# Strassen's scheme for one more stage of a two-layer graph network, its sums of the matrix made in an earlier stage, and another order of products in the last stage

## The chip, the cores and the metric

The kernel runs on one core of one Trainium2 chip. The metric is the device time of one execution in microseconds; "before" is the median of three runs. The profile is one further execution, recorded by the hardware profiler. TensorE (PE in the profile) does matmuls, VectorE (DVE) and ScalarE (ACT) read its results from PSUM, and DMAs are issued from the queues of SyncE (SP), GpSimd (POOL) and ScalarE.

## The reference

Two layers of graph convolution with a residual and a layer norm each. N is 2048 nodes, the batch is 8, and there are 64 features in and out. The weights of each node are mixed from 16 pools by its embedding. Cut to what matters:

```python
def layer0(x, A, emb, weight, bias):
    w = einsum('nd,dkio->nkio', emb, weight); b = emb @ bias
    As = [eye(N), A, 2.0 * (A @ A) - eye(N)]
    x_g = einsum('knm,bmc->bnkc', stack(As), x)
    return einsum('bnki,nkio->bno', x_g, w) + b

def layer1(x, emb, A, weights, bias):
    support = [eye(N), A, 2.0 * A @ A - eye(N),
               softmax(relu(emb @ emb.T), axis=1)]
    ...   # the same two einsums with four supports

x = layernorm(x + layer0(x, adj, ...))
x = layernorm(x + layer1(x, adj, ...))
```

## The kernel before

**Stages.** The work is cut into 40 stages: five phases of eight, each stage for a block of 256 nodes (two slabs of 128). Stage n = 8 i + j is phase i, block j. A0 is u = A x in layer 0, B0 is A u; A1, Z1 and V1 are A x, softmax times x, and A u in layer 1. Stage 8 is thus the first of B0 and stage 32 the first of V1. "Layer 1's s" in the short name of this change is the result of A u there. x and u stay in SBUF, as 16 slabs of 128 nodes by 512 columns (batch times feature). In layer 1, u of a block is stored to memory (`store_u`) and comes back before V1 (`load_u`), since the room of u holds other sums until then.

**Products.** A stage's product is plain or by Strassen's scheme (the variant of Winograd); the set `plain` says which. Plain: 64 units of work; a unit is 128 rows by 128 by 256 columns, and each fp32 matmul of the source is two instructions in the profile. In V1 and B0 the plain form (`turned`) has u stationary and 256 columns of the matrix moving. Strassen (`strassen`): the block of the matrix is cut in four quarters A11 to A22 (slab of rows by parity of the column slab), u or x in four quarters B11 to B22 (parity of slab by left or right half of its columns). Seven products of eight units each make 56 units. In V1 and B0 each product is 32 instructions of 128 moving columns. They are:

```text
p1 = A11 B11   p2 = A12 B21   p3 = (A12-S2) B22   p4 = A22 T4
p5 = (A21+A22) T1   p6 = S2 T2   p7 = (A11-A21) T3     S2 = A21+A22-A11
T1 = B12-B11   T2 = B22-T1   T3 = B22-B12   T4 = T2-B21
c00 = p1+p2   c10 = p1+p6+p7-p4   c11 = p1+p6+p7+p5   c01 = p1+p6+p5+p3
```

c00 and c01 belong to the stage's first slab (slab 0), c10 and c11 to its second (slab 1). Products go to one of two accumulator banks in turn, and a bank is free when the adds that read it are done. The order of products is 1, 4, 7, 2, 6, 5, 3 in every stage.

**Sums.** T1 to T4 are made by VectorE from all slabs of u or x at once, once per phase (`Sums.make`, five operations of 128x2048 or shorter ones). T2 is made in the place of B12. The sums of the quarters of the matrix are made once per block: in stages of A0 with Strassen by `sum_of_a`, and where an A0 stage is plain and its sums are needed later, by `sums_of_a` (four pieces of four VectorE operations of 128x256, and a store of 512 KB on SP for each). Both are stored in `sd` and loaded by later stages. Before, A0's blocks 0 and 1 are plain, as is block 0 of B0, A1 and V1; so only block 1 needs `sums_of_a`.

**Order.** The order of the work around the products is written out by hand: `put(n, place, f, ...)` hangs a call into stage n at a place from 0 to 64, scaled to the stage's length (64 or 56 units); `spread` distributes a list over places. When the product generator has come to a place, the calls are emitted, and every engine works through its instructions in the order of emission. Into each stage's product go: `weights` (matmuls pw, whose results ScalarE and VectorE copy to `w`), `apply` of the stage before (four of them, 32 matmuls po each, for four groups of 32 nodes; the instructions in the profile are twice as many; VectorE accumulates each in four operations by a mask), `post` (mean, square, deviation, scaling, and the output DMA; `post(0)` to `post(2)`), `turn`, loads and stores. The applies of a stage need its result t, in V1 those of slab 1 (2 and 3) first. In the last stage, 39, there is no stage behind: `apply(2)` is at place 60, and 3, 0 and 1 follow behind the products with all of `post`.

**Matrix loads.** `Ahead` keeps four 512 KB buffers of the matrix loaded in the order in which the products use them; each `next()` fills one and takes one. Weights have three such buffers. Both are issued on SP's queue, where an issue that waits for a buffer holds those behind it.

Of the kernel before, what the change touches and what calls it, by code (L numbers as in the profile page):

```python
# [15 lines left out]
P = 128  # L16
# [32 lines left out]
def two_graph_layers(ctx: ExitStack, tc: tile.TileContext, x, x_t, adj_b, adj_q, layers, out):  # L49
# [167 lines left out]
        for q in range(4):  # L217
            pool.dma_start(out=s1[q * D:(q + 1) * D, :].bitcast(F32), in_=estk[1][(q // 2) * D:(q // 2 + 1) * D, :])

    plain = {("A0", 1)} | {(phase, 0) for phase in ("A0", "B0", "A1", "V1")}  # L220

    class Ahead:

# [16 lines left out]
    def load_adj(t, key):  # L240
# [6 lines left out]
        else:  # L247
            sp.dma_start(out=t, in_=src.rearrange("p k n -> p (k n)"))


    lefts = [("quarter", (0, 0)), ("quarter", (1, 1)), ("sum", 2), ("quarter", (0, 1)), ("sum", 1), ("sum", 0), ("sum", 3)]
    quarters = [("quarter", at) for at in ((0, 0), (1, 1), (1, 0), (0, 1))]
    adj = Ahead(4, lambda: stream.tile([P, 4 * NB], F32, tag="a", name="a"), load_adj,
                [key for phase in ("A0", "B0", "A1", "V1") for j in range(NBLK)
                 for key in ([("plain", j, i) for i in range(NJ // 4)] if (phase, j) in plain
                             else [(kind, j, i) for kind, i in (quarters if phase == "A0" else lefts)])])
# [5 lines left out]
    class Stage:  # L262
# [152 lines left out]
        def product(self):  # L415
            if self.wide:
                if self.j % 2 == 0:
                    self.rest = self.pair[1].rest = self.strassen(X)
                    return islice(self.rest, self.length)
                return self.rest  # L420
            if self.phase == "Z1":
                return self.turned(X, self.softmax())
            if self.kk:
                return self.turned(U, self.loaded()) if self.plain else self.strassen(U)
            if self.n == 0:
                self.slabs = U[0:SB]
# [9 lines left out]

        def loaded(self):
            for _ in range(NJ // 4):
                a = adj.next().rearrange("p (m n) -> p m n", n=NB)
                yield [a[:, i, :] for i in range(4)]  # L440

        def accumulator(self, name):
# [15 lines left out]
            self.store_u()  # L458

        def store_u(self):  # L460
            if self.kk == 0:
                for s in range(SB):
                    (sp if self.li else pool).dma_start(out=ud[self.j][:, s, :], in_=self.slabs[s])

        def strassen(self, right):
# [4 lines left out]
                      "B22": lambda k: right[2 * k + 1][:, half:BC]}  # L470
            for i in range(4):
                rights[f"T{i + 1}"] = lambda k, i=i: sums[i](k)
            if self.wide:
                p1, p4, v = (four.tile([P, BC], F32, tag="f2k", name="temp") for _ in range(3))
                mine = {f"A{h + 1}{t + 1}": self.pair[h].quarters[t] for h in range(2) for t in range(2)}
            else:
                temps = one.tile([P, 4, half], F32, tag="wsplit", name="temps")
                p1, p4, v = (temps[:, i, :] for i in range(3))
                mine = {}
            made = {}  # L480
# [4 lines left out]
            def quarter(name):  # L485
                if streamed:
                    mine[name] = adj.next()
                    adj.held += 1
# [6 lines left out]
            def times(name, what, left):  # L495
                made[name] = acc = self.accumulator(name)[:, 0:2 * nodes]
                a = (mine[left] if inside else adj.next()).rearrange("p (k n) -> p k n", n=nodes)
                for k in range(k_slab):
                    if self.kk:
                        for q in range(2):  # L500
                            pe.matmul(acc[:, q * nodes:(q + 1) * nodes], rights[what](k)[:, q * P:(q + 1) * P],
                                      a[:, k, :], start=(k == 0 and q == 0), stop=(k == k_slab - 1 and q == 1))
                            yield nodes / NB
                    else:
                        pe.matmul(acc, a[:, k, :], rights[what](k), start=(k == 0), stop=(k == k_slab - 1))
                        yield 1
                if inside and name in ("p7", "p6", "p5", "p3"):
                    if streamed:
                        adj.held -= 1
                        adj.fill()  # L510
                    self.used(what)

            def add(dst, a, b, op=ALU.add):

# [4 lines left out]
                else:  # L519
# [4 lines left out]
                    for par in range(2):  # L524
                        of = lambda x: x[64 * par:64 * par + 64, :].rearrange("p (q n) -> p n q", n=nodes)
                        dve.tensor_tensor(to[:, :, 4 * dst[1] + par:4 * dst[1] + par + 3:2], of(a), of(b), op=op)

            if inside:
                quarter("A11")
                quarter("A22")  # L530
            yield from times("p1", "B11", "A11")
            act.copy(p1, made["p1"])
            if inside:
                quarter("A21")
                sum_of_a(2, "A11", "A11", "A21", ALU.subtract)
                sum_of_a(0, "A21", "A21", "A22", ALU.add)
            yield from times("p4", "T4", "A22")
            self.used("T4")
            act.copy(p4, made["p4"])
            if inside:  # L540
                quarter("A12")
                sum_of_a(1, "A22", "A22", "A11", ALU.subtract)
            yield from times("p7", "T3", "A11")
            add(v, made["p7"], p1)
            add(p4, v, p4, ALU.subtract)
            yield from times("p2", "B21", "A12")
            add((0, 0), made["p2"], p1)
            if inside:
                sum_of_a(3, "A12", "A12", "A22", ALU.subtract)
            yield from times("p6", "T2", "A22")  # L550
            add(v, made["p6"], v)
            add(p1, made["p6"], p1)
            add((1, 0), made["p6"], p4)
            yield from times("p5", "T1", "A21")
            add(p1, made["p5"], p1)
            add((1, 1), made["p5"], v)
            self.repeat(1)
            yield from times("p3", "B22", "A12")
            add((0, 1), made["p3"], p1)
            self.repeat(0)  # L560
            self.store_u()

# [198 lines left out]
    for c in range(V0 // 8):  # L761
        put(26 + c, 10, load_weights, 1, 1, c)
        for part in range(3):
            put(26 + c, 40 + part, split_weights, part, 1, 1, c)
    for i, place in ((0, 51), (3, 54), (2, 60)):
        put(8, place, sums["B0"].make, i)
    put(9, 0, sums["B0"].make, 1)
    for i, place in enumerate((16, 24, 30, 52)):
        put(1, place, sums["A0"].make, i)
    put(8, 2, load_u, (NBLK - 1,))  # L770
    for i, place in ((0, 20), (3, 24), (2, 32)):
        put(16, place, sums["A1"].make, i, 0, 7)
        put(16, 50, sums["A1"].make, i, 7, 8)
    put(17, 10, sums["A1"].make, 1)
    for i, place in ((0, 10), (2, 20), (3, 30)):
        put(32, place, sums["V1"].make, i)
    put(33, 0, sums["V1"].make, 1)
    for n, st in enumerate(stages):
        phase = st.phase
        cuts = (0, 3, 6, 9, 12, 14, 16) if st.units == C else (0, 3, 6, 8)  # L780
# [5 lines left out]
        if phase == "A0":  # L786
# [2 lines left out]
            spread(n + 1, 1, 31, weights)  # L789
            turned, bursts, posts = 33, (38, 38, 38, 38), (50,)  # L790
        elif phase == "B0":
            if st.j == 7:
                spread(n, 38, 54, weights)
                bursts, posts = (0, 0, 6, 10), ()
                put(n + 1, 16, st.load_x, range(SB))
                for k in range(6):
                    put(n + 1, (11 if k < 3 else 12.5) + 0.5 * k, st.post, k % 3, 8 - k // 3 * 8, 16 - k // 3 * 8)
            else:
                spread(n + 1, 3, 13, weights)
                bursts, posts = (19, 19, 29, 29), (38, 46.5, 50)  # L800
                put(n + 2, 5, st.load_x, range(SB))
        elif phase == "A1":
            spread(n + 1, 12, 34.5, weights)
            turned, bursts, posts = 4, (43, 43, 43, 43), (56,)
            for s, h, place in ((0, 0, 38), (0, 1, 40), (1, 0, 57), (1, 1, 60)):
                put(*((n, place) if st.j or s == 0 else (n + 1, place - 43)), st.scores_of_rows, s, h)
            put(n, 41, st.statistics, 0)
            put(*((n, 62) if st.j else (n + 1, 19)), st.statistics, 1)
            put(n + 1, 24, st.store_c)
        elif phase == "V1":  # L810
            spread(n, (22 if st.j else 4), (62 if st.j < 7 else 52), weights)
            bursts, posts = (4, 4, 4, 4), (15, 19, 23)
            put(n, 20, st.load_z)
        if bursts and n + 1 < len(stages):
# [35 lines left out]
                    put(n, 8 * (c - 3), st.scores, c)  # L850

    last = stages[-1]
    put(len(stages) - 1, 60, last.apply, 2)
    for n, st in enumerate(stages):
        done = 0
        todo = sorted(plans[n])
# [65 lines left out]
```

## Time and profile before

| | us |
|---|---|
| median of 3 runs (1473.73 to 1474.06) | 1473.86 |
| the profiled execution | 1472.41 |
| its span, first to last instruction | 1470.6 |
| TensorE busy | 1446.2 |
| VectorE busy | 952.9 |
| ScalarE busy | 478.5 |
| mean granted TensorE clock | 0.996 |

In the profile's rows "p" is a Strassen accumulator, "pz" a plain one, "pw" the weights, "po" an apply; `p<-a,u` is a matmul into p with the matrix and u. "L43" is the line of a helper through which all instructions go, so that one goes by tile names. A timeline row has its start, its length over all instructions merged in it, the engine, the operation, the tiles and the count; in brackets the idle time ahead of it and what ended that. A row of stretches has the bounds, the length, and then the busy time of TensorE, its weight loads, VectorE, ScalarE and GpSimd, with the granted clock, the DMA engines' share and GB/s.

### The profile page before, as it was taken

The numbers are of one execution on the slowest core, as the hardware profiler recorded it, in microseconds if no ns is written. First come the engines' busy times: TensorE is split into PE (matmuls) and PEld (weight loads), VectorE is DVE, ScalarE is ACT, GpSimd is POOL, SyncE is SP. The second block draws the span as 40 slices with busy tenths as digits, with TensorE's granted clock in tenths as the row PEclk, the third lists the DMA queues.
The fourth block names the chain that finished last, engine by engine and source line by source line (L and its number), as shares of the span: only waits on it lengthen the run. The fifth ranks groups of instructions, "written<-read, shape, count | busy, mean of one in ns | idle before, by whom it ended". The sixth has DMA issues, their size and how long they took to land.

```text
span 1470.6 us, 31139 instructions
## 1 busy us (share of the span) xinstructions
PE 1446.2 (98%) x13310; PEld 1182.1 (80%) x13310; DVE 952.9 (65%) x1611; ACT 478.5 (33%) x594; POOL 205.4 (14%) x341
## 2 busy tenths in 40 slices
PE   9999999999999999999999999999999999999996
PEld 4577777778999998567877777788888888888885
DVE  3866666637666766865666667568783466666666
ACT  1444444432211213154444444432110233333332
POOL 5212221110111111111011111111000000000100
PEclk9999999999999999999999999999999999999998
DMA  9878888884666666477877878212213756665551
GB/s 359 279 260 273 286 284 266 275 316 158 206 191 205 205 205 194 159 176 196 194 197 190 180 212 209 52 51 79 69 58 107 218 180 198 192 188 192 192 188 57
DMA packets 86570, 282.85 MB, mean 192 GB/s; under 512 B 13984, under 2 KB 18080, under 8 KB 84832
## 3 DMA queue, kind: packets, MB, share of 16 engines
q1 hardware_dynamic: 53600, 171.99, 39.0%
q0 software_dynamic: 27360, 95.24, 21.1%
q10 hardware_dynamic: 5472, 13.63, 2.8%
q8 instruction: 105, 1.72, 0.5%
q14 instruction: 33, 0.27, 0.1%
HBM read 216.28 MB, written 60.83 MB: 188 GB/s over the span
## 4 chain that ended last, share of the span: by engine, by line
PE 92%; DVE 4%; issue 2%; DMA 1%; ACT 1%; ACTq 0%; DVEq 0%
PE p L43 56%; PE po L43 13%; PE pw L43 9%; PE pz L43 7%; PE pu L43 4%; PE pt L43 1%; DVE acc L43 1%; PE ps L43 1%; DVE u L43 1%; PE pr L43 1%; DMA x<-in_x 1%; DVE w L43 1%; ACT w L43 0%; ACT sq L43 0%; DVE t L43 0%
## 5 line engine op out<-in xcount | busy, mean ns | idle before, releaser
L43 ACT ACTIVATE w<-pw 128x1024 f32<-128x1024 f32 x330 | 320.1, 1022 | 434.9 <-PE pw L43 433.0
L43 DVE SCALAR_TENSOR_TENSOR acc<-po,mask,acc 128x256 f32<-128x256 f32 (+1 forms) x640 | 247.0, 426 | 74.4 <-PE po L43 57.3
L43 DVE COPY w<-pw 128x1024 f32<-128x1024 f32 x118 | 144.4, 1224 | 150.6 <-PE pw L43 150.3
L43 PE MATMUL p<-a,u 128*128 128x128 f32 x1792 | 219.0, 278 | 0.2 <-issue 0.2
L43 PEld LDWEIGHTS p<-a,u 128*128 128x128 f32 x1792 | 206.6, 192 | 8.1 <-issue 2.2
L43 PE MATMUL po<-w,t 128*32 128x256 f32 (+1 forms) x5120 | 206.2, 337 | 6.2 <-issue 6.2
L43 PE MATMUL p<-u,a 128*128 128x256 f32 x832 | 204.3, 388 | 0.0
L43 PEld LDWEIGHTS po<-w,t 128*32 128x32 f32 (+1 forms) x5120 | 127.2, 108 | 78.7 <-issue 16.2
L43 PEld LDWEIGHTS p<-u,a 128*128 128x128 f32 x832 | 151.6, 190 | 29.2 <-issue 5.4
L43 PE MATMUL p<-x,a 128*128 128x256 f32 x624 | 152.4, 384 | 0.0
L43 PEld LDWEIGHTS pw<-e,wst 64*128 64x128 f32 x1728 | 112.5, 184 | 45.5 <-issue 22.3
L43 PE MATMUL pw<-e,wst 64*128 64x256 f32 x1728 | 146.9, 297 | 2.0 <-ACT w L43 1.1
L43 PEld LDWEIGHTS p<-x,a 128*128 128x128 f32 x624 | 114.7, 190 | 19.3 <-issue 0.5
L43 PE MATMUL pu<-x,a 128*128 128x512 f32 x192 | 88.0, 606 | 0.4 <-DMA x<-in_x 0.3
L43 PE MATMUL p<-w,u 128*128 128x256 f32 x384 | 85.8, 379 | 0.0
L43 PE MATMUL p<-a,w 128*128 128x128 f32 x672 | 81.6, 277 | 0.0
L43 PE MATMUL p<-a,x 128*128 128x128 f32 x672 | 81.0, 277 | 0.0
L43 PEld LDWEIGHTS p<-w,u 128*128 128x128 f32 x384 | 72.1, 190 | 9.3
L43 PEld LDWEIGHTS p<-a,w 128*128 128x128 f32 x672 | 77.4, 192 | 2.6 <-issue 1.4
L43 PEld LDWEIGHTS p<-a,x 128*128 128x128 f32 x672 | 77.2, 192 | 1.9
L43 ACT ACTIVATE sq<-acc 128x1024 f32<-128x1024 f32 (+2 forms) x19 | 17.5, 922 | 159.0 <-DVE acc L43 146.4
L43 PEld LDWEIGHTS pu<-x,a 128*128 128x128 f32 x192 | 35.4, 192 | 41.7 <-issue 37.4
(123 smaller groups left out, 1435.5 us busy)
## 6 DMA issues: line engine op xcount, KB each, us to landing
wst<-wd SPq DMA_DIRECT2D x108, 512.0 KB, 6.4
a<-in_adj_q SPq DMA_DIRECT2D x87, 512.0 KB, 5.8
a<-sd SPq DMA_DIRECT2D x84, 512.0 KB, 4.2
sd<-a POOLq DMA_DIRECT2D x24, 512.0 KB, 6.2
a<-in_adj_b SPq DMA_DIRECT2D x16, 512.0 KB, 6.6
bx<-bx POOLq DMA_DIRECT2D x32, 256.0 KB, 5.4
acc<-bx POOLq DMA_DIRECT2D x16, 512.0 KB, 7.1
pd<-acc POOLq DMA_DIRECT2D x16, 512.0 KB, 4.7
```

The source lines that it names most:

```text
L43: return self._tc.keep_in_program_order(f(*args, **kwargs))
```

## The change

Four things, which hang together.

- Stage 32 (V1, block 0) is taken out of `plain`. It runs Strassen's scheme in the order 1, 2, 3, 4, 7, 6, 5, so that the three products with u's own quarters come ahead of those with sums. Its T sums are made at places 2, 6, 16 and 26 of the same stage (before: T1, T4, T3 at 10, 20, 30 of stage 32, T2 at the start of stage 33).
- The sums of the matrix for block 0 are made by `sums_of_a` in stage 8, at places 10, 26, 36 and 57. B0's T3 and T2 move from place 60 of stage 8 and 0 of stage 9 to places 1 and 10 of stage 9.
- Stage 7 (A0's last block) writes its u into slabs 14 and 15 of u itself. Its stores to memory and its load in stage 8 go.
- Stage 39 (V1's last) runs in the order 1, 4, 7, 6, 5, 2, 3, so that slab 1 is done after five products. Applies 2 and 3 go to place 50, the first parts of slab 1's `post` to 58 and 61; its weights run from place 12 to 42 instead of 22 to 52.

The diff, cut to its core:

```diff
-    plain = {("A0", 1)} | {(phase, 0) for phase in ("A0", "B0", "A1", "V1")}
+    plain = {("A0", 0), ("A0", 1), ("B0", 0), ("A1", 0)}
+
+    factors = {1: (("quarter", (0, 0)), "A11", "B11"), 2: (("quarter", (0, 1)), "A12", "B21"), 3: (("sum", 3), "A12", "B22"),
+               4: (("quarter", (1, 1)), "A22", "T4"), 5: (("sum", 0), "A21", "T1"), 6: (("sum", 1), "A22", "T2"),
+               7: (("sum", 2), "A11", "T3")}
+    orders = {("V1", 0): (1, 2, 3, 4, 7, 6, 5), ("V1", NBLK - 1): (1, 4, 7, 6, 5, 2, 3)}
+    usual = (1, 4, 7, 2, 6, 5, 3)
...
-            if self.n == 0:
-                self.slabs = U[0:SB]
+            if self.n == 0 or (self.phase, self.j) == ("A0", NBLK - 1):
+                self.slabs = U[SB * self.j:SB * self.j + SB]
...
-            if self.kk == 0:
+            if self.kk == 0 and self.slabs[0] is not U[-SB]:
                 for s in range(SB):
                     (sp if self.li else pool).dma_start(out=ud[self.j][:, s, :], in_=self.slabs[s])
...
+            for p in order:
+                acc = yield from times(p)
...
+                elif p == 2:
+                    add(c00, acc, w1)
...
+                elif p == 6:
+                    add(v, acc, v)
+                    u2 = w1 if order[-1] != 3 or order == usual else more
+                    add(u2, acc, w1)
+                    if order[-1] != 3:
+                        add(more, more, u2)
+                    add(c10, acc, w4)
+                elif p == 5:
+                    if order[-1] == 3:
+                        add(u2, acc, u2)
+                    else:
+                        add(c01, acc, more)
+                    add(c11, acc, v)
+                    self.repeat(1)
+                elif order[-1] == 3:
+                    add(c01, acc, u2)
+                else:
+                    act.copy(more, acc)
...
-    for i, place in ((0, 51), (3, 54), (2, 60)):
-        put(8, place, sums["B0"].make, i)
-    put(9, 0, sums["B0"].make, 1)
+    for i, (n, place) in ((0, (8, 51)), (3, (8, 54)), (2, (9, 1)), (1, (9, 10))):
+        put(n, place, sums["B0"].make, i)
...
-    put(8, 2, load_u, (NBLK - 1,))
...
-    for i, place in ((0, 10), (2, 20), (3, 30)):
+    for i, place in ((0, 2), (3, 6), (2, 16), (1, 26)):
         put(32, place, sums["V1"].make, i)
-    put(33, 0, sums["V1"].make, 1)
...
         elif phase == "B0":
+            for c in range(NJ // 4 if st.j == 0 else 0):
+                put(n, (10, 26, 36, 57)[c], st.sums_of_a, c)
...
-            spread(n, (22 if st.j else 4), (62 if st.j < 7 else 52), weights)
+            spread(n, (22 if 0 < st.j < 7 else 12 if st.j else 4), (62 if st.j < 7 else 42), weights)
...
-    put(len(stages) - 1, 60, last.apply, 2)
+    for c in (2, 3):
+        put(len(stages) - 1, 50, last.apply, c)
+    for part, place in enumerate((58, 61)):
+        put(len(stages) - 1, place, last.post, part, 8, 16)
...
-    for c in (3, 0, 1):
-        last.apply(c)
-        if c == 0:
-            last.post(0, 8, 16)
-            last.post(1, 8, 16)
-    for part, g0, g1 in ((0, 0, 4), (2, 8, 16), (1, 0, 4), (0, 4, 8), (2, 0, 4), (1, 4, 8), (2, 4, 8)):
+    last.post(2, 8, 16)
+    last.apply(0)
+    last.post(0, 0, 4)
+    last.apply(1)
+    for part, g0, g1 in ((1, 0, 4), (0, 4, 8), (2, 0, 4), (1, 4, 8), (2, 4, 8)):
         last.post(part, g0, g1)
```

More of the change, by code (lines that the diff above doesn't have):

```diff
@@ L248, in load_adj @@
             sp.dma_start(out=t, in_=src.rearrange("p k n -> p (k n)"))
-    lefts = [("quarter", (0, 0)), ("quarter", (1, 1)), ("sum", 2), ("quarter", (0, 1)), ("sum", 1), ("sum", 0), ("sum", 3)]
     quarters = [("quarter", at) for at in ((0, 0), (1, 1), (1, 0), (0, 1))]
@@ L255, in two_graph_layers @@
                  for key in ([("plain", j, i) for i in range(NJ // 4)] if (phase, j) in plain
-                             else [(kind, j, i) for kind, i in (quarters if phase == "A0" else lefts)])])
+                             else [(kind, j, i) for kind, i in (quarters if phase == "A0" else
+                                                           [factors[p][0] for p in orders.get((phase, j), usual)])])])
     wst = Ahead(3, lambda: three.tile([P, 8, P], F32R, tag="wst", name="wst"),
@@ L438, in loaded @@
             for _ in range(NJ // 4):
-                a = adj.next().rearrange("p (m n) -> p m n", n=NB)
+                self.a = a = adj.next().rearrange("p (m n) -> p m n", n=NB)
                 yield [a[:, i, :] for i in range(4)]
@@ L472, in strassen @@
                 rights[f"T{i + 1}"] = lambda k, i=i: sums[i](k)
+            order = orders.get((self.phase, self.j), usual)
             if self.wide:
-                p1, p4, v = (four.tile([P, BC], F32, tag="f2k", name="temp") for _ in range(3))
+                temps = [four.tile([P, BC], F32, tag="f2k", name="temp") for _ in range(3)]
                 mine = {f"A{h + 1}{t + 1}": self.pair[h].quarters[t] for h in range(2) for t in range(2)}
             else:
-                temps = one.tile([P, 4, half], F32, tag="wsplit", name="temps")
-                p1, p4, v = (temps[:, i, :] for i in range(3))
+                room = one.tile([P, 4, half], F32, tag="wsplit", name="temps")
+                temps = [room[:, i, :] for i in range(4)]
                 mine = {}
-            made = {}
             nodes = NB if self.wide else P
@@ L493, in sum_of_a, with times @@
                     pool.dma_start(out=sd[self.j][i].rearrange("p k n -> p (k n)"), in_=mine[name])
-            def times(name, what, left):
-                made[name] = acc = self.accumulator(name)[:, 0:2 * nodes]
+            def times(p):
+                _, left, what = factors[p]
+                acc = self.accumulator(f"p{p}")[:, 0:2 * nodes]
                 a = (mine[left] if inside else adj.next()).rearrange("p (k n) -> p k n", n=nodes)
                 for k in range(k_slab):
+                    start, stop = k == 0, k == k_slab - 1
                     if self.kk:
@@ L501, in times @@
                             pe.matmul(acc[:, q * nodes:(q + 1) * nodes], rights[what](k)[:, q * P:(q + 1) * P],
-                                      a[:, k, :], start=(k == 0 and q == 0), stop=(k == k_slab - 1 and q == 1))
+                                      a[:, k, :], start=(start and q == 0), stop=(stop and q == 1))
                             yield nodes / NB
                     else:
-                        pe.matmul(acc, a[:, k, :], rights[what](k), start=(k == 0), stop=(k == k_slab - 1))
+                        pe.matmul(acc, a[:, k, :], rights[what](k), start=start, stop=stop)
                         yield 1
[L507 to L511, printed above, removed]
+                return acc
             def add(dst, a, b, op=ALU.add):
@@ L526, in add @@
                         dve.tensor_tensor(to[:, :, 4 * dst[1] + par:4 * dst[1] + par + 3:2], of(a), of(b), op=op)
+            c00, c01, c10, c11 = (0, 0), (0, 1), (1, 0), (1, 1)
+            w1, w4, v = temps[:3]
+            more = temps[-1]
             if inside:
@@ L530, in strassen @@
                 quarter("A22")
[L531 to L559, printed above, removed]
+            for p in order:
+                acc = yield from times(p)
+                if inside and p in (7, 6, 5, 3) and streamed:
+                    adj.held -= 1
+                    adj.fill()
+                self.used(factors[p][2])
+                if p == 1:
+                    act.copy(w1, acc)
+                    if inside:
+                        quarter("A21")
+                        sum_of_a(2, "A11", "A11", "A21", ALU.subtract)
+                        sum_of_a(0, "A21", "A21", "A22", ALU.add)
+                elif p == 4:
+                    act.copy(w4, acc)
+                    if inside:
+                        quarter("A12")
+                        sum_of_a(1, "A22", "A22", "A11", ALU.subtract)
+                elif p == 7:
+                    add(v, acc, w1)
+                    add(w4, v, w4, ALU.subtract)
+                elif p == 2:
+                    add(c00, acc, w1)
+                    if inside:
+                        sum_of_a(3, "A12", "A12", "A22", ALU.subtract)
+                elif p == 6:
[16 more added lines that the diff above has]
+                    act.copy(more, acc)
```

## The prediction

> **What bounds the kernel now.** I read the first page from the top, then the chain of waits, then two places of the timeline: stage 32, where the change swaps a scheme, and the last 25 us.
>
> ```profile
> span 1470.6 us, 31139 instructions
> PE 1446.2 (98%) x13310; PEld 1182.1 (80%) x13310; DVE 952.9 (65%) x1611; ACT 478.5 (33%) x594; POOL 205.4 (14%) x341
> PE 92%; DVE 4%; issue 2%; DMA 1%; ACT 1%; ACTq 0%; DVEq 0%
> ```
>
> TensorE is busy for 1446.2 of 1470.6 us. Of the 24.4 us left, about 14 lie before the first product and 13.7 after the last matmul. So between them it hardly ever waits, and a change can gain in two ways only: less TensorE work, or a shorter tail. It can lose wherever it makes TensorE wait.
>
> The stretches of three stages (us; then each engine's busy time, granted clock, DMA share) and of the end:
>
> ```profile
> 1148.40:1182.16 33.76, 33.76 (x194) 27.97 (x193) 17.16 (x12) 10.50 (x12) 3.28 (x7) 1.00 0.60 187
> 1182.16:1220.40 38.24, 38.24 (x418) 33.72 (x417) 26.01 (x40) 14.43 (x17) 3.18 (x5) 1.00 0.62 197
> 1220.40:1258.60 38.20, 38.20 (x419) 33.69 (x418) 24.07 (x41) 12.75 (x16) 3.37 (x6) 1.00 0.62 197
> 1457.00:1463.00 6.00, 0.00 (x0) 0.00 (x0) 5.01 (x12) 0.93 (x2) 0.00 (x0) 0.78 0.00 0
> 1463.00:1470.00 7.00, 0.00 (x0) 0.00 (x0) 3.95 (x12) 1.43 (x4) 0.00 (x0) 0.50 0.33 75
> ```
>
> Row one is stage 32, with plain products and no applies; rows two and three are stages 33 and 34, with Strassen's products and four applies. All have TensorE full at clock 1.00. The last rows show the tail: TensorE idle, VectorE at work.
>
> **The change part by part.**
>
> *Stage 32's products.* 128 plain instructions of 256 columns become 224 of 128 columns. The cost of the new form is read off stage 34: 38.20 us, of which the chain gives the applies 7.04:
>
> ```profile
> 1222.08 7.04 PE po L43 x128
> ```
>
> 31.16 us are left, with the same 64 weight matmuls (pw) as stage 32. Against 33.76 that saves 2.60 us. A rule speaks against the exchange: the Trainium skill, "TensorE: Matmul & The Clock Gate", section "Back-to-back issue gap", says that in a stream of weight load and matmul pairs, narrow matmuls are spaced wider than their columns need, 81 ns instead of 56 for 128 columns in its case, 1.45 times. By that factor the 224 instructions would take 37 us instead of about 26, and the stage would lose some 9 us. This trace has 64 instructions of 128 columns in 7.34 us (0.1147 each) and 24 of 256 columns in 5.38 us (0.224 each): two narrow ones cost 1.02 times a wide one. I take the trace.
>
> *Its sums move ahead of its products.* VectorE in stage 32 before, and the loads of u on SP's queue:
>
> ```profile
> 1148.60 1.39 DVE L43 TENSOR_TENSOR t<-p,temp 64x512 f32<-64x512 f32 x2 [4.79 <-PE p L43]
> 1151.01 1.22 DVE L43 COPY w<-pw 128x1024 f32<-128x1024 f32 x1 [1.01 <-PE pw L43]
> 1152.26 2.29 DVE L43 TENSOR_TENSOR x<-u 128x2048 f32<-128x2048 f32 x1
> ...
> 1110.61 31.40 SPq L43 DMA_DIRECT2D u<-ud  x8
> ```
>
> Seen here: a sum of 2048 columns takes 2.29 us, a copy of weights 1.22, and the last u load is issued at about 1141.7; these loads take 3.1 to 4.7 us to land, so u is whole by 1146.4. The new order in VectorE's queue is: stage 31's last adds to 1150.0; T1 to 1152.3; copy to 1153.5; T4 (two sums) to 1158.1; copy to 1159.4; T3 to 1161.7; p2's add c00 (two of 0.42) to 1162.5. TensorE: p1, p2 and p3 are 24 units, 96 instructions x 0.1147 = 11.0 us, plus three groups of weights of 0.90: p4 is due at 1162.1. T4 is in time by 4 us, but p4 accumulates in the bank of p2 (there are two), and c00 frees it at 1162.5 only. Cost: about 0.5 us. Bounds: 0 if the adds are granted earlier, 2.3 if one more sum gets in front. T3, T2 and T1 are needed from unit 32 on and are cheap there; T2 leaves stage 33, where VectorE had slack (no gain: rows two and three differ by 0.04 us). POOL's issues are not held: in before, t<-zd and acc<-pd issued in 0.52 and 0.57 us inside a sum.
>
> *End of stage 32.* p5 now comes last and ends two results, c01 and c11: four adds of 0.42, so slab 1 is ready 0.2 + 1.7 = 1.9 us behind the last product, plus 0.1. The applies of stage 33 begin with slab 1, after 14 instructions of p1 (1.6 us). Wait: 0.35 us (0 to 0.8).
>
> *Loads.* Stage 32 takes seven 512 KB blocks of the matrix instead of four. Three are loaded long before, each further one is issued three products (11 us and more) ahead and lands in 4 to 6 us. Nothing. If that cover were gone, each late block would cost up to 6 us.
>
> *Stage 8: sums of the matrix, made for stage 32.* Sixteen VectorE operations of 128x256, 0.42 us each, 6.7 us in four pieces, with four 512 KB stores on SP. VectorE there:
>
> ```profile
> 334.85 7.89 DVE L43 SCALAR_TENSOR_TENSOR acc<-po,mask,acc 128x256 f32<-128x256 f32 x16 [2.67 <-PE po L43]
> 342.66 2.28 DVE L43 TENSOR_TENSOR w<-u 128x2048 f32<-128x2048 f32 x1
> ...
> 350.11 2.27 DVE L43 TENSOR_TENSOR w<-u 128x2048 f32<-128x2048 f32 x1
> 352.31 0.68 DVE L43 COPY t<-pz 64x512 f32<-64x512 f32 x1
> 352.91 2.27 DVE L43 TENSOR_TENSOR u<-u,w 128x2048 f32<-128x2048 f32 x1
> 355.11 2.41 DVE L43 COPY w<-pw 128x1024 f32<-128x1024 f32 x2
> ```
>
> Pieces 0 and 1 fall into idle time (VectorE stood 9.6 us ahead of 321.5 and 8.0 us ahead of 330.8), piece 2 behind the turn's copies: 332.2 to 333.9, just ahead of the applies' 334.85. Its buffer is free if the store of piece 1, issued near 324.5, lands within 7.7 us; the four such stores in stage 1 took 3.7 to 8.3, median 4.1. Piece 3 adds 1.7 us behind T1 and T4, but T2 (2.27) moves behind the copies at 355.1, so these start where they did. On SP, the store of piece 3 waits for VectorE until 351.9 with the next matrix load behind it; that load was issued at 351.4 and is needed 12 us later. Cost 0.1 us: below nothing is hardly possible, as TensorE has no wait there to give back beyond 0.4 us; above, 1.2 us if the store of piece 1 is slow.
>
> *Stage 7 writes its u in place.* Two stores of 256 KB on POOL and one load of 512 KB on SP go. SP stood at that load until 318.7; nobody on TensorE waited for what was behind it. Zero.
>
> *Stage 39 and the tail.* Before, one apply lies inside the products and three behind; VectorE ends the run:
>
> ```profile
> 1453.57 3.99 DVE L43 SCALAR_TENSOR_TENSOR acc<-po,mask,acc 128x256 f32<-128x256 f32 x8 [0.81 <-PE po L43]
> ...
> 1460.43 2.03 DVE L43 SCALAR_TENSOR_TENSOR acc<-po,mask,acc 128x256 f32<-128x256 f32 x4
> ...
> 1467.09 0.43 DVE L43 TENSOR_TENSOR acc<-acc,rstd 128x256 f32<-128x256 f32 x1
> ```
>
> After: applies 2 and 3 at unit 43.75. Up to the end of p3, TensorE has the same work as before less two applies of 1.76: it ends at 1456.96 - 3.5 = 1453.4. From unit 43.75 on that is 12.25 units (5.6) and two applies (3.5), so they start at 1444.3. VectorE: eight accumulations 1446.3 to 1450.3, c00 to 1451.15, first part of post (0.68 + 0.17 + 0.69) to 1452.75, the square on ScalarE to 1453.5, the reduction to 1454.2, c01 to 1455.05. Apply 0 may start at 1455.15; its accumulation starts 2.0 behind, 1457.15 to 1459.2; post of its half 1.05; accumulation of apply 1, 2.0, to 1462.2. What then remains ran from 1464.21 to 1467.52 before, 3.3 us: the end is at 1465.5, 2.05 earlier. The output of 128 KB follows as before. The weights start ten places earlier at the same spacing; their last block, issued at about unit 17 and needed at unit 31, has 8.7 us against 6.4 that such loads take to land: zero, and up to 2 if it is late. Gain 2.05; bounds 0.5 (VectorE behind by one more step at c01) and 2.6 (no delay of c01).
>
> **Sum.** -2.60 + 0.5 + 0.35 + 0.1 - 2.05 = -3.7 us. The profiled execution took 1472.41 us (its span 1470.6), 1.45 below the median of the runs, 1473.86. The same difference on the median gives 1470.2 us. About 0.2%, 2.95 us, is what a measurement of this kernel can tell from no change.
>
> **The rivals.**
>
> *No new wait shows.* p4's bank, the start of stage 33 and c01 all come in time: 2.6 + 2.6 = 5.2 us, 1468.6. For it: the waits I worked out are each half a microsecond. Against: VectorE's queue is strict in both places. 0.15.
>
> *VectorE takes back more than half.* It is the bound in the tail now and would be fed faster: c01 slips, and in stage 32 one more sum lies ahead of c00 (p4 1.5 late). Gain 0.5 in the tail and 0.8 in stages 8, 32 and 33, 1.3 in all at the far end, and up to 2.9: around 1471.8, within what can be told. For it: VectorE is the only engine at work in the tail rows. Against: the bounds are the far ends. 0.28.
>
> *u comes late for stage 32: slower.* The plain products need slabs 4 to 7, which are loaded last, only in the second quarter; p1 needs slab 4 with its third pair, 0.9 us in, and T1 all of u. Every microsecond after 1150.0 goes through T1, T4, T3 and c00 to p4. The gain is gone at 1153.7, a landing 12.0 us behind the issue, and from 15.0 us on (2.95 more) the loss can be told: 1476.8. Landings here were 3.1 to 4.7, so it is unlikely. I give 0.07 to this and to the like at stage 8.
>
> **How the numbers follow.** Forecast (gain 3.0 to 4.6, 1469.3 to 1470.9) 0.50, no new wait 0.15, VectorE takes back 0.28, slower 0.07. Faster is the first two, 0.65. The range reaches from the no-wait case with a little over it, 1468.3, to most of the third, 1472.6.
>
> **What would show it.** In the changed profile: 96 more TensorE instructions; stage 32 at 31 to 32 us, with a gap below 1 us before p4 and one below 0.5 ahead of stage 33's applies; the copies of weights in stage 9 still near 355; a gap of about 1.7 us on TensorE behind the last product, until c01 is there; and from the first apply matmul in stage 39 (1412.96) to the end of VectorE's last operation (1467.52) 52.6 us instead of 54.6. Wrong would be: narrow products at more than 0.12 us each, a wait of TensorE for a u load at the start of stage 32, or that last stretch shortened by less than 1 us.

## The result, and the profile after

| | before | after |
|---|---|---|
| median of 8 runs each, us | 1473.91 | 1469.12 |
| lowest to highest, us | 1472.76 to 1475.75 | 1468.35 to 1470.69 |
| span of the profiled execution, us | 1470.6 | 1466.6 |
| TensorE busy, us | 1446.2 | 1443.3 |

The ratio is 0.9968, with a 95% interval from 0.9957 to 0.9979: 3 to 6 us faster. The forecast was 1470.2. Later the changed kernel was timed twice more, on two chips, with 0.9966 (0.9955 to 0.9976) and 0.9961 (0.9948 to 0.9973).

The first page of the profile after, the lines that answer to those of before:

```profile
span 1466.6 us, 31370 instructions
PE 1443.3 (98%) x13406; PEld 1184.7 (81%) x13406; DVE 962.8 (66%) x1638; ACT 478.1 (33%) x595; POOL 204.4 (14%) x339
PE 93%; DVE 3%; DMA 2%; issue 1%; ACT 1%; ACTq 0%; DVEq 0%
```

TensorE has the 96 instructions more that were counted, and 2.9 us less to do. The stretch of stage 32, and VectorE in it (timeline):

```profile
1148.79:1179.90 31.11, 31.11 (x289) 29.59 (x288) 22.23 (x21) 10.68 (x13) 3.08 (x6) 1.00 0.78 253
```

```profile
1150.41 2.29 DVE L43 TENSOR_TENSOR x<-u 128x2048 f32<-128x2048 f32 x1
...
1156.19 2.29 DVE L43 TENSOR_TENSOR x<-x,u 128x2048 f32<-128x2048 f32 x1
...
1161.74 0.86 DVE L43 TENSOR_TENSOR t<-p,temps 64x256 f32<-64x256 f32 x2
...
1162.70 4.72 PE L43 MATMUL p<-a,x 128*128 128x128 f32 x40
```

31.11 us instead of 33.76, all of it busy at full clock. T1 starts at 1150.41, T4 ends at 1158.5, and c00, the two adds of p2, at 1162.60. p4, the first product with T sums, begins at 1162.70: it came due just as its bank came free. Where stage 33 begins (TensorE, timeline):

```profile
1179.90 1.73 PE L43 MATMUL p<-a,u 128*128 128x128 f32 x14
1181.94 7.11 PE L43 MATMUL po<-w,t 128*32 128x256 f32 x128 [0.31 <-issue]
```

```profile
1180.10 1.73 DVE L43 TENSOR_TENSOR t<-p,temps 64x256 f32<-64x256 f32 x4 [2.46 <-PE p L43]
```

The 14 instructions ahead of the applies end, and 0.31 us pass. The trace names no cause for this wait ("issue"), but VectorE's four adds of c01 and c11 end at 1181.83, 0.1 us before the applies start: slab 1 was not there sooner. Stage 9, VectorE:

```profile
351.27 0.42 DVE L43 TENSOR_TENSOR sums<-a,sums 128x256 f32<-128x256 f32 x1
...
354.40 1.21 DVE L43 COPY w<-pw 128x1024 f32<-128x1024 f32 x1
...
357.50 2.28 DVE L43 TENSOR_TENSOR u<-u,w 128x2048 f32<-128x2048 f32 x1
```

Piece 3 of the matrix sums ends at 351.7, the first copy of weights starts at 354.4 (355.1 before), and T2 comes behind the second. TensorE there, in the profile before and in the one after:

```profile
355.51 1.36 PE L43 MATMUL pw<-e,wst 64*128 64x256 f32 x12
```

```profile
355.57 0.98 PE L43 MATMUL pw<-e,wst 64*128 64x256 f32 x12
```

These twelve weight matmuls had short waits in them before, which are gone. The end:

```profile
1452.40 0.86 DVE L43 TENSOR_TENSOR t<-p,temps 64x256 f32<-64x256 f32 x2
1453.32 3.66 PE L43 MATMUL po<-w,t 128*32 128x256 f32 x64 [1.57 <-DVE t L43]
1458.40 2.03 DVE L43 SCALAR_TENSOR_TENSOR acc<-po,mask,acc 128x256 f32<-128x256 f32 x4
...
1463.23 0.42 DVE L43 TENSOR_TENSOR acc<-acc,rstd 128x256 f32<-128x256 f32 x1
```

c01 is the first row, TensorE's gap of 1.57 us in wait for it the second. From the first apply matmul in stage 39 (1412.89 before, 1411.01 after) to the end of the last VectorE operation it was 54.63 us and is 52.64.

### The profile page after: what moved, and what is told of

It is laid out like the page before. It is cut to its first block, busy times and chain, and to the rows that moved or that the text cites. A ratio compares the mean times of both kernels' runs of the same rounds, so it can differ in the third digit from the quotient of the medians.

```text
span 1466.6 us, 31370 instructions
## 1 busy us (share of the span) xinstructions
PE 1443.3 (98%) x13406; PEld 1184.7 (81%) x13406; DVE 962.8 (66%) x1638; ACT 478.1 (33%) x595; POOL 204.4 (14%) x339
## 4 chain that ended last, share of the span: by engine, by line
PE 93%; DVE 3%; DMA 2%; issue 1%; ACT 1%; ACTq 0%; DVEq 0%
PE p L43 57%; PE po L43 14%; PE pw L43 9%; PE pz L43 6%; PE pu L43 4%; PE pt L43 1%; DMA wst<-wd 1%; PE ps L43 1%; PE pr L43 1%; DVE acc L43 1%; DVE u L43 1%; DMA x<-in_x 1%; DVE mean L43 0%; ACT w L43 0%; DVE t L43 0%
## 5 line engine op out<-in xcount | busy, mean ns | idle before, releaser
L43 PE MATMUL p<-a,u 128*128 128x128 f32 x1920 | 233.7, 278 | 0.8 <-issue 0.8
L43 PEld LDWEIGHTS p<-a,u 128*128 128x128 f32 x1920 | 221.1, 192 | 8.9 <-issue 2.7
L43 PE MATMUL p<-a,x 128*128 128x128 f32 x768 | 93.0, 277 | 0.0
L43 PEld LDWEIGHTS p<-a,x 128*128 128x128 f32 x768 | 88.3, 192 | 2.4
```

The source lines that it names most:

```text
L43: return self._tc.keep_in_program_order(f(*args, **kwargs))
```

## The experiments

**The two halves of the change.** The first three kernels were timed on one chip, together with a second run of the changed one (1470.91). First, the old last stage (its places and the end of the kernel as before, too) with everything else new:

```diff
-    orders = {("V1", 0): (1, 2, 3, 4, 7, 6, 5), ("V1", NBLK - 1): (1, 4, 7, 6, 5, 2, 3)}
+    orders = {("V1", 0): (1, 2, 3, 4, 7, 6, 5)}
...
```

> The changed kernel with stage 39 and everything behind it as before (order 1, 4, 7, 2, 6, 5, 3, apply 2 at place 60, the rest behind the products, weights from 22 to 52). My theory: stage 32 gives 2.65 us and the start of stage 33 takes 0.35 back, the tail gave 2.0 and is gone here. So about 2.3 to 2.8 us faster than before (1471.1 to 1471.6), 2.0 slower than the change; from the first apply of stage 39 to VectorE's last operation 54.6 us again. Rival, the tail is the whole gain: no difference from before. Rival, the tail gives nothing on the clock because the output's landing sets the end: as fast as the change (1469.1).

Measured: 0.9976 (0.9966 to 0.9987) of before, 1.9 to 5.0 us faster. Stage 32 took 31.12 us, the last stretch 54.6. Second, stage 32 plain again, with V1's T sums at their places of before and no sums of the matrix in stage 8; the new last stage stays, and so do the places of B0's T3 and T2 and the u of stage 7 in place:

```diff
-    plain = {("A0", 0), ("A0", 1), ("B0", 0), ("A1", 0)}
+    plain = {("A0", 0), ("A0", 1), ("B0", 0), ("A1", 0), ("V1", 0)}
...
-            for c in range(NJ // 4 if st.j == 0 else 0):
-                put(n, (10, 26, 36, 57)[c], st.sums_of_a, c)
...
```

> Stage 32 plain again with its T sums at the old places, and no sums of the matrix in stage 8; the new stage 39 and tail, the places of B0's T3 and T2 and the u of stage 7 in place remain. My theory: 2.0 us from the tail and 0.3 from stage 9, where one copy of weights is no longer behind two sums: about 2.0 to 2.4 us faster than before (1471.5 to 1471.9), stage 32 at 33.76 us. Rival, the tail gives nothing: as before. Rival, the tail gives all: as fast as the change.

Measured: 0.9974 (0.9964 to 0.9984), stage 32 at 33.75 us, the last stretch 52.61. Each half alone is faster than before, so neither is without effect. That neither is the whole, the times alone hardly tell: the medians of both lie 1.6 us above the changed kernel's, but the intervals overlap (0.9955 to 0.9976 for the change). The profiles tell it, since in each kernel the one stretch has the new length and the other the old. In time the halves give some 3.5 and 3.8 us, more than 2.3 to 2.8 and 2.0 to 2.4, with intervals that reach down to 1.9 and 2.4; the profiles, which resolve these stretches to 0.1 us, have the expected sizes.

**Stage 8's sums by themselves.** As the kernel before this, but with the four pieces in stage 8.

> As tail_only, but with the sums of the matrix made and stored in stage 8 (nobody reads them). It prices stage 8's part alone. My theory: hidden, within 0.2 us of tail_only in the span, the copies of weights in stage 9 later by 1.7 us less what fits ahead of them, TensorE's gap there below 0.3 us. Rival, VectorE is the bound at this stage boundary: 1.2 us slower than tail_only. Rival, 2 MB more of stores slow the other transfers: waits for weight loads (wst) show on TensorE.

Measured: 0.9977 (0.9970 to 0.9984), no different from tail_only. From the applies in stage 8 to the first ones in stage 9, both profiles take 0.34 us less than the one of before: the 6.7 us of VectorE work cost TensorE nothing. They are hidden, as the prediction had it, and stage 9 even gains, since T2 moved away. The waits for weight loads, which one rival named, were 4.5 us here and 3.2 in tail_only, but in stages 18 to 23, long after these stores.

**The spread between profiles.**

> The changed kernel as it is. In its first profile it ran 1.6 us ahead of before between stages 9 and 16 and lost 1.5 of that between stages 19 and 23, where nothing was changed, with two waits of TensorE for weight loads. My theory: these are run-to-run differences of transfers; the second profile shows other amounts in these stages, while stage 32 (31.1 us), the gap ahead of stage 33's applies (0.3 to 0.5) and the last stretch (52.6) are the same to 0.1. Rival, they belong to the change (SP's order of loads): the same 1.6 and 1.5 us again.

> The kernel before, for a second profile. In all four profiles of changed kernels so far TensorE waited 1.2 to 4.5 us for weight loads (wst) in stages 18 to 23, in the one of before it did not. My theory: these waits come and go with the landing of these loads from run to run and have nothing to do with the change; this profile shows between 0 and 4 us of them as well. Rival, the change brought them: none here.

> The changed kernel on this chip, to compare the other three with. Expected 0.30 to 0.35% below before, last stretch 52.6, stage 32 31.1 us, a gap of 0.3 to 0.5 ahead of stage 33's applies, waits for weight loads between 0 and 4 us.

At the first applies behind B0 the first profile of the change is 1.2 us ahead of before and the others 1.0 and 0.8. Only some 0.5 us of this lead are made in stages 7 to 9; the rest comes and goes, since u_late and post1_behind_c01, which are the same kernel in these stages, are 0.4 and 0.5 us behind before there. The second profile has waits of 2.3 us for weight loads (first 1.2), the third none, and the second profile of before has 0.4. Of the kernels timed with the second profile, old_tail had 2.0, tail_only 3.2 and tail_and_sums8 4.5; of the later ones none had more than 0.2. In the five profiles with such waits in stages 18 to 23 the slowest weight load took 13.6 to 14.5 us to land (from 690 to 930 us), in the other nine 11.7 to 12.8. So the waits come with slow loads, and the changed kernel has profiles of both kinds; why the loads of these five were slow stays open. Between stage 10 and stage 32, where the change does nothing, the first changed profile lost 0.7 us in all (0.3 ahead of before to 0.4 behind), which is most of why its span gained 4.0 and the changed stretches together 4.7. The last stretch is 52.6 in all profiles of the change, the gap ahead of stage 33's applies 0.30 to 0.31.

**The order with u's own quarters first.**

```diff
-    orders = {("V1", 0): (1, 2, 3, 4, 7, 6, 5), ("V1", NBLK - 1): (1, 4, 7, 6, 5, 2, 3)}
+    orders = {("V1", NBLK - 1): (1, 4, 7, 6, 5, 2, 3)}
```

> Stage 32 by Strassen's scheme, but in the order of all other stages (1, 4, 7, 2, 6, 5, 3) with T1 to T4 at the same places. It tests the part of the change that puts u's own quarters first. My theory: T4 is ready about 1158.5 on the clock of the changed profile, since VectorE has stage 31's adds, T1 (2.3), a copy (1.2) and T4 (4.6) in front, and p4 would begin after 8 units at 1153.4: TensorE waits 5.1 us there and nowhere else, stage 32 takes 36.2 instead of 31.1 us, the kernel is 5 us slower than the change and about as before (1473.5 to 1474.5 where the change has 1469.1). Rival, the order is of no weight because the sums are in time anyway: as the change. Rival, T3 and T2 are late too: another 2 to 4 us.

Measured: 1.0034 (1.0023 to 1.0045): slower than before, and 9 to 10 us slower than the change. TensorE and VectorE in stage 32 (timeline), then the stretches ahead of, with and behind the lower clock (it is the third figure from the end):

```profile
1157.44 4.54 PE L43 MATMUL p<-a,x 128*128 128x128 f32 x24 [5.02 <-DVE x L43]
...
1162.69 1.22 DVE L43 COPY w<-pw 128x1024 f32<-128x1024 f32 x1 [5.40 <-PE pw L43]
1163.83 2.28 DVE L43 TENSOR_TENSOR x<-u 128x2048 f32<-128x2048 f32 x1
...
1166.26 3.81 PE L43 MATMUL p<-a,x 128*128 128x128 f32 x32 [2.29 <-DVE x L43]
```

```profile
1154.21:1157.62 3.41, 0.18 (x1) 0.21 (x2) 3.05 (x2) 0.00 (x0) 0.00 (x0) 1.00 0.98 221
1157.62:1161.03 3.41, 3.41 (x18) 3.41 (x17) 0.00 (x0) 0.00 (x0) 0.00 (x0) 0.50 0.68 245
1161.03:1164.45 3.42, 2.94 (x28) 2.50 (x27) 1.76 (x2) 2.00 (x3) 0.00 (x0) 1.00 0.28 89
```

The expected wait for T4 is there to 0.1 us. So is the one of the rival, for a later sum (2.29). Here the two queues hold each other: in VectorE's queue T3 (1163.83) stands behind a copy of weights, for which VectorE waited 5.40 us, because TensorE made these weights only after its own wait for T4. And then there is a third part that neither expectation had: behind the wait the clock stood at 0.50 for 3.41 us, 1.7 us of work lost. From the start of stage 32 to the applies of stage 33 the profiles are 9.1 us apart, of which 5.02 + 2.29 + 1.7 - 0.3 (no gap in stage 33) explain 8.7. The order is thus not a refinement: without it the first half of the change loses.

**u too late.** The rival of the prediction that ended slower, forced. The first trial moved the last two loads of u behind the last product of stage 31 in the order of emission, onto ScalarE's queue.

> The last two loads of u (slabs 4 to 7) are issued on ScalarE's queue behind the last product of stage 31 instead of on SP's behind the one before it, about 7 us later. It prices the rival that ended slower in the prediction. My theory: they land 4 to 5 us behind 1148.8; p1 of stage 32 does two of its eight pairs and waits about 3 to 4 us for slab 4, T1 starts as much later, and the waits are not paid twice because products and sums shift together: 3 to 4 us slower than the change. In the change itself the same loads had some 2 us to spare. Rival, VectorE's chain adds its own delay at p4: 6 us and more slower, beyond before. Rival, hidden: no difference.

It tells nothing of a late u. ScalarE's queue was empty, so the loads went out at 1138.6 and 1142.4 as in the change, and the time was that of the change (0.9967, 0.9955 to 0.9980): a later place in the program is no later issue where nothing on that queue waits. In the changed kernel these loads land 3.6 to 4.0 us after the issue, at about 1146, 4 us ahead of T1. The second trial put a copy of p3's result in front:

```diff
+                    if self.wide and self.j == NBLK - 2:
+                        act.copy(v, acc)
+                        self.used("late")   # load_u of slabs 4 to 7, on ScalarE's queue
                     add(c01, acc, u2)
```

> The experiment u_late once more: there the loads went out as early as before (1138.6 and 1142.4), because nothing on ScalarE's queue held them. Now a copy of p3's result on ScalarE (0.6 us, unused) stands ahead of them, so they are issued about 1149.7 and 1150.1 where stage 32 begins at 1148.8. My theory: they land at about 1153.5 to 1154.5, p1 waits 3 to 4.5 us for slab 4, T1 starts as much later than 1150.4, later products do not wait once more (0.5 at most ahead of p4), and the kernel is 3 to 5 us slower than the change, about as before. Rival, VectorE's chain adds its own delay at p4: 6 us and more slower than the change. Rival, hidden: no difference.

Measured: 1.0011 (1.0003 to 1.0020), some 7 us slower than the change; in the profiles 6.5, from the start of stage 32 to the applies of stage 33. TensorE waits (timeline), and the clock:

```profile
1152.85 1.23 PE L43 MATMUL p<-a,u 128*128 128x128 f32 x4 [2.89 <-DMA u<-ud]
1154.39 0.79 PE L43 MATMUL p<-a,u 128*128 128x128 f32 x2 [0.31 <-DMA u<-ud]
```

```profile
1149.14:1152.55 3.41, 0.82 (x8) 0.63 (x6) 1.38 (x2) 0.55 (x1) 1.14 (x3) 1.00 0.65 247
1152.55:1159.38 6.83, 6.21 (x30) 5.47 (x31) 4.82 (x3) 1.94 (x2) 1.53 (x3) 0.50 0.91 201
1159.38:1163.00 3.62, 3.62 (x34) 3.50 (x34) 3.19 (x2) 0.37 (x1) 0.00 (x0) 1.00 0.92 269
```

The waits are 3.2 us, within what I expected; the size is the rival's, but not by its mechanism. There is no further wait ahead of p4. Instead the clock is at 0.50 for 6.83 us, in which TensorE was busy for 6.21: 3.1 us of work lost.

**The places of B0's T3 and T2.**

```diff
-    for i, (n, place) in ((0, (8, 51)), (3, (8, 54)), (2, (9, 1)), (1, (9, 10))):
+    for i, (n, place) in ((0, (8, 51)), (3, (8, 54)), (2, (8, 60)), (1, (9, 0))):
```

> The changed kernel with B0's T3 and T2 at their old places (60 of stage 8, 0 of stage 9), the sums of the matrix in stage 8 stay. It prices the move of these two, which by the prediction makes room for piece 3. My theory: VectorE has piece 3 (1.7 us) and both T sums ahead of the first copy of weights of stage 9, which starts 1.7 us later than in the kernel before and 2.4 us later than in the change; three buffers of weights' results absorb about 0.5; TensorE waits 1.5 to 2 us in stage 9, the kernel is that much slower than the change. Rival, the copies have slack: no wait, as the change.

Measured: 0.9984 (0.9978 to 0.9991), about 3.4 us slower than the change on the same chip; in the profiles 3.6 from the applies of stage 8 to the first ones of stage 9. TensorE waits three times (timeline), and is slowed behind that:

```profile
356.26 0.50 PE L43 MATMUL pw<-e,wst 64*128 64x256 f32 x4 [0.63 <-ACT w L43]
357.17 0.50 PE L43 MATMUL pw<-e,wst 64*128 64x256 f32 x4 [0.41 <-ACT w L43]
358.09 0.51 PE L43 MATMUL pw<-e,wst 64*128 64x256 f32 x4 [0.41 <-ACT w L43]
```

```profile
355.84:359.25 3.41, 2.17 (x18) 1.62 (x19) 3.10 (x3) 2.47 (x4) 1.21 (x3) 1.00 0.78 186
359.25:362.67 3.42, 3.42 (x20) 3.20 (x21) 0.00 (x0) 1.01 (x2) 0.00 (x0) 0.50 1.01 373
362.67:366.00 3.33, 3.33 (x55) 3.07 (x59) 1.23 (x1) 1.40 (x2) 1.06 (x2) 1.00 0.72 251
```

The waits are 1.45 us, just below the expected 1.5 to 2; 1.7 us more are the clock, at 0.50 for 3.42 us; some 0.4 us of the 3.6 are not resolved. So stage 8's sums are free only because T3 moved behind the last turned copy and T2 behind two copies of weights.

**Trying for more.** First the part of the tail where VectorE held c01 back:

```diff
-    for part, place in enumerate((58, 61)):
-        put(len(stages) - 1, place, last.post, part, 8, 16)
+    put(len(stages) - 1, 58, last.post, 0, 8, 16)
...
+    last.post(1, 8, 16)
     last.post(2, 8, 16)
```

> In the last stage the second part of slab 1's post (the reduction of the squares) goes behind c01 on VectorE instead of ahead of it. My theory: c01 starts when the last product ends (0.2 behind it) instead of 0.5 to 0.7 later, TensorE's gap behind the last product shrinks from 1.57 to about 1.1 us, the moved part fits into VectorE's wait for apply 0 (1.1 us), and the last stretch takes 52.1 instead of 52.6 us. On the clock 0.5 us, not to be told from the change. Rival, VectorE is full there: the stretch stays at 52.6 or more because the moved part delays the accumulation of apply 0.

Measured: 0.9965 (0.9953 to 0.9977). TensorE's gap and the stretch, 51.98 us (1410.34 to 1462.32):

```profile
1452.00 3.66 PE L43 MATMUL po<-w,t 128*32 128x256 f32 x64 [0.95 <-DVE t L43]
```

0.95 instead of 1.57, and 0.66 us less in the stretch: that part of the wait was VectorE's order, as reasoned. What is left are c01's two adds themselves, 0.85 us. The times can't tell it from the change. Then three edits at once, meant as the faster version: the one above, the applies and first weights of stage 33 at place 5, and

```diff
-            spread(n + 1, 12, 34.5, weights)
+            spread(n + 1, 9, 35.5, weights)
...
```

> The change with three more edits: the second part of slab 1's post behind c01 (as in post1_behind_c01), the applies and the first weights of stage 33 one place later, and the weights of layer 1's A1 stages spread from place 9 to 35.5 instead of 12 to 34.5, so that the last weight load has 1.2 us more before its use. My theory: the last stretch 52.0, no gap ahead of stage 33's applies (0.35 less), waits for weight loads in stages 18 to 23 near zero whatever they are for the change on this chip (up to 4 us): 1 to 3 us faster than the change. Rival, the earlier start of the weights meets the turn's copies on ScalarE and VectorE and costs up to 0.5 us in each of eight stages: slower than the change.

Measured: 1.0025 (1.0017 to 1.0033), the rival, and worse than its 0.5. The earlier weights lose about 1.04 us in each of the stages from 18 to 23, and some in those beside them. VectorE and TensorE in stage 18, where TensorE needs the third buffer of weights' results:

```profile
676.57 1.39 DVE L43 COPY t<-pt 64x512 f32<-64x512 f32 x2 [3.45 <-ACT t L43]
...
678.11 0.50 PE L43 MATMUL pw<-e,wst 64*128 64x256 f32 x4 [0.77 <-DVE t L43]
```

The turn's copies, on ScalarE behind the statistics and then on VectorE, hold that buffer until 677.96. The other two edits did in place what was meant: no gap ahead of stage 33's applies, last stretch 52.0. But in this profile the kernel gained 0.4 us on the change by the applies of stage 34 and lost 0.6 by those of stage 35, with a wait of 0.42 us at the start of stage 34 (also seen, 0.75, in one profile of the change). So a gain is shown for the last stretch alone, 0.6 us. A version with these two and without the weights' move was not run.

## Why the prediction was right

| step | forecast, us | in the profile, us |
|---|---|---|
| stage 32's products | -2.60 | -2.65 |
| p4 waits for its bank | +0.5 | 0 |
| start of stage 33 | +0.35 | +0.31 |
| stages 8 and 9 | +0.1 | -0.34 |
| tail | -2.05 | -1.99 |
| sum | -3.7 | -4.7 |

The medians differ by 4.8, just above the 3.0 to 4.6 that the forecast was given and towards the rival without any new wait (5.2). The mechanisms, the cover in stage 8 included, were the right ones; that stage 32 gave a little more than was forecast is luck, as the second point shows.

- Narrow products: stage 32 took what stage 34 had shown, less the applies (31.11 us for 31.16). The rule that narrow matmuls are spaced wider, from the Trainium skill's "TensorE: Matmul & The Clock Gate", section "Back-to-back issue gap", would by the estimate of the prediction have made the stage some 9 us longer, and it became 2.65 shorter: the rule does not hold for these instructions, and the trace was the better guide.
- p4's bank was the mis-sized term. From the start of the stage I had c00 done after 14.1 us and p4 due after 13.7. It was 13.8 and 13.9: two small errors met, and the wait of 0.5 became none. A margin of 0.1 us is luck. The order of events in VectorE's queue was as worked out, step by step.
- Stage 9: I expected the copies of weights to start where they did. They started 0.7 earlier: piece 3 took 1.5 us (350.15 to 351.7) where T2, which left, had taken 2.2. I had both numbers and took them as equal. TensorE's waits for these copies' buffers, 0.38 us within twelve matmuls (1.36 to 0.98), went with it; tail_only shows the same gain without the pieces.
- Stage 7, which the table leaves out, was not quite zero. The load of u on SP held the weight load behind it until 319.1; after the change that load goes out at 314.1. TensorE stood near 325 in both profiles of before (0.1 and 0.4 us, in the second by the trace for that load) and in no profile of a changed kernel, so the stretch from the applies of stage 7 to those of stage 8 is 0.2 us shorter in the profile after.
- One reading of the first page was wrong, without effect on the sum. The 14 us ahead of the first product are not idle: TensorE stands for at most 1.4 of them. Of its 24.4 idle us, 13.7 lie behind the last matmul and some 9 in between, most of it ahead of applies in stages 10 to 15.
- The tail came out as worked, to 0.2: gap 1.57 for 1.7, stretch 52.64 for 52.6. post1_behind_c01 shows that 0.6 of that gap was VectorE's order.
- The rivals: a full gain without any wait was nearly it in stage 32, but c01's gap stayed. VectorE as the one that takes back is real, yet only in other orders (usual_order32, old_t_places8). The late u I priced microsecond for microsecond; u_late2 shows 6.5 us for 3.2 us of waiting. From which delay on the gain is gone was not run.

## What to carry to other kernels

Where one engine is full, the new cost of its stage is best read from a neighbouring stage that already works in the new form, and the hidden work must be laid into the other engines' queues in order, since a sum of durations would not tell the good order (31.1 us) from the usual one (9 us slower). A cover that holds by 0.1 us is luck, so look at what was moved to make it: here the T sums' places and the order of products are each worth more than the scheme itself (3.4 and 9 us against 2.65). On a full TensorE a wait can cost twice its length, because the clock may be lower behind it: 3.2 us of waiting cost 6.5 here, and 1.45 cost 3.6.

## What the runs showed of the hardware that I had not expected

A wait well below what I thought necessary lowers the clock. In these traces the granted clock is 1.00 or 0.50 and nothing between, and each time it falls ahead of the end of the run it stays at 0.50 for 3.41 us, or for twice that in u_late2. In old_tail a single gap of 1.82 us, in stage 15, was enough; in u_late the same place had one of 1.54 us and the clock stayed at 1.00 (stretches of old_tail, then of u_late):

```profile
566.08:569.49 3.41, 1.58 (x40) 1.20 (x46) 1.23 (x4) 0.00 (x0) 0.00 (x0) 1.00 0.53 187
569.49:572.90 3.41, 3.41 (x117) 3.00 (x99) 1.92 (x8) 0.00 (x0) 0.00 (x0) 0.50 0.02 5
```

```profile
569.07:572.49 3.42, 1.92 (x117) 1.73 (x117) 0.81 (x4) 0.00 (x0) 0.00 (x0) 1.00 0.46 159
572.49:576.00 3.51, 3.22 (x30) 3.14 (x28) 3.42 (x14) 0.00 (x0) 0.00 (x0) 1.00 0.00 0
```

The length of one gap does not decide: three gaps of 0.63, 0.41 and 0.41 us within 3 us lowered the clock (old_t_places8), a single one of 1.57 in the tail of the change and one of 0.77 in the last experiment did not. Nor does the busy time of the 3.41 us ahead, as this profile counts it: the clock fell behind 2.17 us of it (old_t_places8) and did not behind 1.92 (u_late). What decides, these runs do not settle. The Trainium skill, "TensorE: Matmul & The Clock Gate", section "What's actually happening", has the clock halve after an idle window of about 3.4 us; only in usual_order32 was a gap that long (5.02), and by that rule the waits of old_t_places8 and u_late2 would have cost their own 1.45 and 3.2 us, where 3.6 and 6.5 were measured.
